# Spectra loads in the places of the copied products, tied to blocks, in the product stage of a two-layer MetaFormer kernel

## The chip, the cores and the metric

The kernel runs on one core of one Trainium2 chip. The metric is the device time in microseconds of one execution; the median of several is compared. The engines go by the profile's names: PE (TensorE matmuls), PEld (its weight loads), DVE (VectorE), ACT (ScalarE), POOL (GpSimd) and SP (SyncE, which here only issues DMAs).

## What is computed

The input is 16 images of 128 channels by 32 x 32, float32. Two layers follow each other, each a token mixer and a channel mixer with residual additions. Layer 0 is linear attention, then a spectral unit; layer 1 is a pair of 3 x 3 convolutions, then a routed feed-forward part with 64 experts. The stage that the change touches is the core of the spectral unit:

```python
Vf = jnp.fft.rfft(phi, n=n, axis=0)
Uf_p = jnp.fft.rfft(u, n=n, axis=1)
Uf_m = jnp.fft.rfft(u * sgn3, n=n, axis=1)
U_plus = jnp.fft.irfft(Vf[None, :, :, None] * Uf_p[:, :, None, :], n=n, axis=1)[:, :sl]
U_minus = jnp.fft.irfft(Vf[None, :, :, None] * Uf_m[:, :, None, :], n=n, axis=1)[:, :sl]
...
out = jnp.einsum('btkd,k,kde->bte', U_plus, s, Mpp)
out = out + jnp.einsum('btkd,k,kde->bte', U_minus, s, Mpm)
```

For every frequency the kernel forms one 128 x 128 complex matrix g, the sum over the filters of filter spectrum times mixing matrix, and multiplies the spectra of all 16 samples with it. That multiplication, frequency by frequency, is the product stage.

## The kernel before

Four stages follow each other: attention and forward transform of layer 0 (lines 220 to 773), the product stage (lines 776 to 896), the inverse transform with convolutions and routing of layer 1, and the expert part with the output. The forward transform leaves the spectra in a DRAM tensor `vd`; the product stage reads them from there and writes its results to the DRAM tensors `yd`, from which the next stage loads.

The product stage works in NCH = 16 chunks of frequencies, and each chunk c in NM = 4 blocks m. What a chunk needs:

- `xc`, the spectra of chunk c, in four loads of 256 KB, one for each four samples (`begin`, line 785; the DMA is line 793). Each has its own place, so the four loads of the next chunk can start as soon as POOL has read the four places.
- `v`, made from them by POOL: for each load two `tensor_tensor` (line 796) and one `tensor_scalar` (line 797) that stores a negated part. This document calls these three instructions "turns". There are two tiles `v`.
- `g`, the matrices of the chunk: `generate` (line 799) makes 16 matmuls on 4 PSUM banks, `collect` (line 810) copies the four banks to SBUF, by ACT (line 818) or DVE (line 816). A chunk needs eight generates. There are two tiles `g`.

A block (c, m) does in this order: two generates for chunk c + 1; the first collect; `combine` of the block before; the second collect; `multiply` (line 820), which writes one PSUM bank `py` with 32 matmuls from `v` and `g` of chunk c; ACT's copy of `py` to the SBUF tile `yt` (line 891). `combine` (line 855) is two DVE instructions (lines 858 and 859) that read `yt` and write sum and difference into `ys`. So the result of a block is combined within the block after it. When the fourth block of a chunk has been combined, `finish` (line 838) does four POOL instructions on `ys` (lines 843 to 846) and SP issues two stores of 512 KB to `yd` (line 850). In block (c, 0) finish of chunk c - 1 thus comes first on POOL, and then the turns for chunk c + 1.

The matmuls are float32; the profile counts two records for each `nc.tensor.matmul`, so a generate pair shows as 64 records and a multiply as 64.

PE, DVE, ACT and POOL run in the order of the program text: that is what `tc.manual_schedule(engines=PINNED)` does. SP is not among the pinned engines, and its order is the framework's: in the steady part the two stores of a chunk come first, then four loads that run one chunk ahead of the turns that POOL is doing, each load issued when POOL has finished with its place. `yt` has one place, the four `xc` have one each, and each of the five takes 2 KB per partition.

Of the kernel before, what the change touches and what calls it, by code (L numbers as in the profile page):

```python
# [8 lines left out]
F32 = mybir.dt.float32  # L9
AF = mybir.ActivationFunctionType  # L10
ALU = mybir.AluOpType
# [3 lines left out]
P = 128  # L15
B, C, H, W = 16, 128, 32, 32
# [15 lines left out]
NM = NQ // 2  # L32
NCH = 16
JL = 8
CW = 2 * 2 * NM * JL

BP = B // 4
# [3 lines left out]
RG = P // KR  # L41
# [4 lines left out]
PINNED = {  # L46
    mybir.EngineType.PE, mybir.EngineType.DVE, mybir.EngineType.Activation, mybir.EngineType.Pool,
}
# [21 lines left out]
def metaformer_kernel(ctx: ExitStack, tc: tile.TileContext, io: dict, out: bass.AP):  # L70
    nc = tc.nc
# [26 lines left out]
    for n, (g_, b_, m_, v_) in enumerate(((V_G1, V_B1, V_M1, V_V1), (V_G2, V_B2, V_M2, V_V2))):  # L98
# [15 lines left out]
                name=nc.get_next_instruction_name(), ins=[], outs=[], act_func_set_id=EXP_LN  # L114
# [61 lines left out]
    with ExitStack() as l0:  # L176
# [3 lines left out]
        vd = dram.tile([NCH, P, B, CW], F32, name="vd", tag="vd")  # L180
# [39 lines left out]
        with ExitStack() as a0:  # L220
# [537 lines left out]
            with tc.manual_schedule(engines=PINNED):  # L758
                for p in range(-reach, B):
                    next(preparing, None)  # L760
                    for name, d in period:
                        b = p + d
# [13 lines left out]
        with ExitStack() as g0:  # L776
            gpl = [g0.enter_context(tc.tile_pool(name="gpl0", bufs=1))]
            cpl = g0.enter_context(tc.tile_pool(name="cpl", bufs=2, reuse_waits="tile"))
            gpl.append(g0.enter_context(tc.tile_pool(name="gpl1", bufs=1, reuse_waits="tile")))
            xcl = g0.enter_context(tc.tile_pool(name="xcl", bufs=1, reuse_waits="tile"))  # L780
            psg = g0.enter_context(tc.tile_pool(name="psg", bufs=8, space=PSUM, reuse_waits="tile"))
            gs, vs = {}, {}
            NB = EPR // 4

            def begin(c):

                v = cpl.tile([P, 2 * NM * JL, 3, B], F32, name="v", tag="v")
                vs[c] = v
                vv = v.rearrange("p (x w) k b -> p x k b w", x=2)
                for i in range(B // BP):  # L790
                    bs = slice(i * BP, (i + 1) * BP)
                    xc = xcl.tile([P, BP, 2, 2, NM * JL], F32, name="xc", tag=f"xc{i}")
                    nc.sync.dma_start(xc.rearrange("p b x r w -> p b (x r w)"), vd[c, :, bs, :])
                    e, o = (xc[:, :, x].rearrange("p b r w -> p r b w") for x in range(2))
                    for x, op in enumerate((ALU.add, ALU.subtract)):
                        nc.gpsimd.tensor_tensor(vv[:, x, 1:, bs], e, o, op)  # L796
                    nc.gpsimd.tensor_scalar(v[:, :, 0, bs], v[:, :, 2, bs], -1.0, None, ALU.mult)  # L797

            def generate(c, q):

                pg = [psg.tile([P, 4, CW], F32, name="pg", tag="p") for r in range(RG)]
                for i in range(4):
                    for r in range(RG):
                        rs = slice(r * KR, (r + 1) * KR)
                        nc.tensor.matmul(  # L805
                            pg[r][:, i], mst[rs, 4 * q + i, :], ph[rs, c, :], start=True, stop=True,
                        )
                return pg

            def collect(c, q, pg):  # L810

                for r in range(RG):
                    dst = gs[c].rearrange("p w (g q i) -> p g q w i", g=RG, q=NB)[:, r, q]
                    src = pg[r].rearrange("p i w -> p w i")
                    if r % 2 and (r == 1 or q % 2 or c == 0):
                        nc.vector.tensor_copy(dst, src)  # L816
                    else:
                        nc.scalar.copy(dst, src)  # L818

            def multiply(c, m, x, py, fresh):  # L820

                g, v = gs[c], vs[c]
                for kl in range(JL // RG):
                    for ri in range(2):
                        for grp in range(RG):
                            jl = RG * kl + grp
                            rows = slice(grp * 2 * B, (grp + 1) * 2 * B)

                            nc.tensor.matmul(  # L829
                                py[rows, x, kl, :],  # L830
                                v[:, (x * NM + m) * JL + jl, 1 - ri : 3 - ri, :]
                                .rearrange("p k b -> p (k b)"),
                                g[:, ((x * 2 + ri) * NM + m) * JL + jl, :],
                                start=(grp not in fresh), stop=(ri == 1), skip_group_check=True,
                            )
                            fresh.add(grp)

            def finish(c, ys):

                eng = nc.gpsimd if c + 1 < NCH else nc.vector  # L840
                e = cpl.tile([P, JL // RG, 2, C], F32, name="ye", tag="ye", bufs=1)
                yv = ys[:, :, 0]
                eng.tensor_tensor(e, yv[:, :, :2], yv[:, :, 2:], ALU.add)  # L843
                eng.tensor_tensor(yv[:, :, 2:], yv[:, :, :2], yv[:, :, 2:], ALU.subtract)  # L844
                eng.tensor_tensor(yv[:, :, 0], e[:, :, 0], e[:, :, 1], ALU.add)
                eng.tensor_tensor(yv[:, :, 1], e[:, :, 0], e[:, :, 1], ALU.subtract)
                for kl in range(JL // RG):
                    last = c + 2 >= NCH
                    j0 = kl * RG + (c - NCH + 2 if last else c) * JL
                    nc.sync.dma_start(  # L850
                        yd[last][j0 : j0 + RG].rearrange("g r b x e -> (g r b) (x e)"),
                        ys[:, kl].rearrange("p x m e -> p (x m e)"),
                    )

            def combine(c, m, ys, t):

                a, b = t
                nc.vector.tensor_tensor(ys[:, :, 0, m], b, a, ALU.add)
                nc.vector.scalar_tensor_tensor(ys[:, :, 1, m], b, -1.0, a, ALU.mult, ALU.add)
                if m == NM - 1:  # L860
                    finish(c, ys)

            with tc.manual_schedule(engines=PINNED):
                begin(0)
                gs[0] = gpl[0].tile([P, CW, C], F32, name="g", tag="g")
                for q in range(NB):
                    collect(0, q, generate(0, q))
                waiting = None
                for c in range(NCH):
                    if c + 1 < NCH:  # L870
                        gs[c + 1] = gpl[(c + 1) % 2].tile([P, CW, C], F32, name="g", tag="g")

                    ys = cpl.tile([P, JL // RG, 2, NM, C], F32, name="ys", tag="ys")
                    for m in range(NM):
                        if c + 1 < NCH:
                            pg = [generate(c + 1, 2 * m + x) for x in range(2)]
                            collect(c + 1, 2 * m, pg[0])
                        if waiting:
                            combine(*waiting)
                        if c + 1 < NCH:  # L880
                            if m == 0:
                                begin(c + 1)
                            collect(c + 1, 2 * m + 1, pg[1])
                        py = psg.tile([P, 2, JL // RG, C], F32, name="py", tag="p")
                        fresh = set()
                        for x in range(2):
                            multiply(c, m, x, py, fresh)
                        if c + 1 < NCH or m == 0:
                            t = cpl.tile([P, 2, JL // RG, C], F32, name="yt", tag="yt", bufs=1)
                        if c + 1 < NCH:  # L890
                            nc.scalar.copy(t, py)
                            waiting = c, m, ys, (t[:, 0], t[:, 1])
                        else:
                            nc.scalar.copy(t[:, m % 2], py[:, 0])
                            waiting = c, m, ys, (t[:, m % 2], py[:, 1])
                combine(*waiting)


    gpool = ctx.enter_context(tc.tile_pool(name="gpool", bufs=1))
# [10 lines left out]
    with ExitStack() as c1:  # L910
# [562 lines left out]
        with tc.manual_schedule(engines=PINNED | {mybir.EngineType.SP}):  # L1473
# [4 lines left out]
            bs = w1[:, C, :].rearrange("(k r i) h -> r k i h", r=2, i=EG)  # L1478
# [137 lines left out]
        with tc.manual_schedule(engines=PINNED):  # L1616
            yt = first.tile([P, 2, N], F32, name="yt", tag="v")
            for pr in (0, 7, 1, 2, 3, 4, 5, 6):
# [8 lines left out]
                for j in range(2):  # L1627
                    b = 2 * pr + j
                    if j and pr % 2:
                        t = yt[:, pr // 2 % 2]  # L1630
# [160 lines left out]
```

## Time and profile before

| what | value |
| --- | --- |
| time, median of 3 executions | 1241.78 us (1241.42 to 1245.75) |
| time of the profiled execution | 1238.85 us |
| its span | 1237.1 us |
| granted TensorE clock, mean | 0.992 |
| line 829, multiply: first start to last start | 395.7 to 652.6 us |
| turns, first to last start | 386.9 to 645.0 us |
| copy of `py` to `yt` (line 891) | 0.586 us |
| combine (lines 858 and 859), median | 0.451 and 0.952 us |
| turns of one load: lines 796, 796, 797, median | 0.741, 0.741 and 0.851 us |
| finish (lines 843 to 846), median | 1.397, 1.268, 0.731 and 0.919 us |
| load of `xc`: KB, issue to landing | 256, 3.4 us (2.9 to 5.6) |
| store to `yd`: KB, issue to landing | 512, 3.6 us |

The span is the time from the first to the last recorded work of that one execution; the device time holds a little more around it. A median over instructions mixes those that run beside others and those that run alone: lines 858 and 859 take from 0.411 to 0.977 us. "Issue to landing" runs from SP's instruction to the last signal of the transfer.

### The profile page before, as it was taken

The numbers are of one execution on the slowest core, as the hardware profiler recorded it, in microseconds if no ns is written. First come the engines' busy times: TensorE is split into PE (matmuls) and PEld (weight loads), VectorE is DVE, ScalarE is ACT, GpSimd is POOL, SyncE is SP. The second block draws the span as 40 slices with busy tenths as digits, with TensorE's granted clock in tenths as the row PEclk, the third lists the DMA queues.
The fourth block names the chain that finished last, engine by engine and source line by source line (L and its number), as shares of the span: only waits on it lengthen the run. The fifth ranks groups of instructions, "written<-read, shape, count | busy, mean of one in ns | idle before, by whom it ended". The sixth has DMA issues, their size and how long they took to land.

```text
span 1237.1 us, 34361 instructions
## 1 busy us (share of the span) xinstructions
PE 1160.6 (94%) x14398; PEld 953.9 (77%) x14398; DVE 936.6 (76%) x1944; ACT 725.1 (59%) x1420; POOL 603.4 (49%) x800
## 2 busy tenths in 40 slices
PE   7889999999999999999997999999999999998996
PEld 6677777777767988988887888898888888885453
DVE  5888888888766777776674689898988989885235
ACT  4777787777655777777770445555555555544211
POOL 2435454655568788888793433343443333230003
PEclk9999999999999999999998999999999999999998
DMA  7005334353436344333348612223233321416899
GB/s 281 24 31 168 120 116 154 97 171 100 154 120 197 98 140 140 128 128 128 108 140 274 153 52 52 85 88 119 84 120 120 103 86 68 154 34 218 323 403 384
DMA packets 91243, 175.14 MB, mean 142 GB/s; under 512 B 5968, under 2 KB 42064, under 8 KB 90448
## 3 DMA queue, kind: packets, MB, share of 16 engines
q1 hardware_dynamic: 90448, 170.46, 41.2%
q0 software_dynamic: 640, 2.49, 0.6%
q8 instruction: 113, 1.85, 0.6%
q14 instruction: 42, 0.34, 0.1%
HBM read 110.28 MB, written 62.65 MB: 140 GB/s over the span
## 4 chain that ended last, share of the span: by engine, by line
PE 38%; DVE 22%; POOL 17%; issue 13%; ACT 5%; DMA 4%; SPq 0%; POOLq 0%; DVEq 0%; ACTq 0%
PE pcv L988 10%; POOL v L796 7%; PE big L638 6%; DVE bst L135 4%; POOL v L797 4%; PE big L171 3%; PE big L152 3%; PE big L570 3%; PE big L450 2%; PE big L533 2%; PE big L432 2%; PE py L829 2%; POOL ye L843 1%; DVE abss L1231 1%; POOL ys L844 1%
## 5 line engine op out<-in xcount | busy, mean ns | idle before, releaser
L988 PE MATMUL pcv<-v,cw 128*128 128x256 f32 x1152 | 258.2, 380 | 1.4 <-POOL v L1178 1.4
L988 PEld LDWEIGHTS pcv<-v,cw 128*128 128x128 f32 x1152 | 214.7, 190 | 34.5 <-issue 4.9
L818 ACT COPY g<-pg 128x512 f32<-128x512 f32 x316 | 161.1, 605 | 45.3 <-PE pg L805 44.6
L816 DVE COPY g<-pg 128x512 f32<-128x512 f32 x196 | 127.7, 682 | 72.0 <-PE pg L805 72.0
L805 PE MATMUL pg<-ph,mst 32*128 32x128 f32 x4096 | 143.0, 279 | 9.4 <-issue 7.9
L805 PEld LDWEIGHTS pg<-ph,mst 32*128 32x128 f32 x4096 | 127.9, 186 | 25.4 <-issue 16.3
L829 PE MATMUL py<-g,v 128*32 128x128 f32 x4096 | 124.8, 274 | 1.9 <-POOL v L797 1.7
L829 PEld LDWEIGHTS py<-g,v 128*32 128x32 f32 x4096 | 108.0, 110 | 9.9 <-POOL v L797 2.3
L144 ACT ACTIVATE tok<-tok,sts 128x128 f32<-128x128 f32 x256 | 101.9, 480 | 16.9 <-DVE sts L1065 13.6
L135 DVE BATCH_NORM_STATS2 bst<-big 128x6 f32<-128x256 f32 x256 | 91.2, 418 | 20.9 <-PE big L152 11.7
L796 POOL TENSOR_TENSOR v<-xc 128x256 f32<-128x256 f32 x128 | 99.0, 798 | 3.3 <-PE pg L805 2.3
L638 PE MATMUL big<-u,mu 128*128 128x128 f32 (+4 forms) x384 | 86.0, 380 | 0.0
L1178 POOL TENSOR_TENSOR v<-abss 128x256 f32<-128x256 f32 x64 | 49.1, 787 | 68.1 <-DVE abss L1174 56.7
L286 POOL TENSOR_TENSOR xf<-ab 128x256 f32<-128x256 f32 x34 | 24.8, 728 | 110.2 <-DVE ab L253 110.2
L1197 POOL TENSOR_TENSOR yo<-abss 128x256 f32<-128x256 f32 x32 | 23.5, 735 | 108.6 <-DVE abss L1193 108.6
L638 PEld LDWEIGHTS big<-u,mu 128*128 128x128 f32 x384 | 56.7, 191 | 18.0 <-issue 15.4
L570 PE MATMUL big<-wf,ub 128*128 128x256 f32 x256 | 62.0, 385 | 0.2
L144 ACT ACTIVATE tt<-tt,sts 128x128 f32<-128x128 f32 x128 | 51.1, 481 | 14.6 <-DVE sts L1065 14.6
L797 POOL TENSOR_SCALAR v<-v 128x256 f32<-128x256 f32 x64 | 55.6, 868 | 5.6
L475 POOL TENSOR_TENSOR ke<-ke,ks 128x1024 f32<-128x1024 f32 x16 | 30.6, 1914 | 55.1 <-DVE qs L483 43.4
L570 PEld LDWEIGHTS big<-wf,ub 128*128 128x128 f32 x256 | 46.2, 190 | 8.8 <-ACT xn L423 3.0
L144 ACT ACTIVATE ub<-ub,sts 128x128 f32<-128x128 f32 x128 | 50.8, 481 | 0.0
(256 smaller groups left out, 2478.9 us busy)
## 6 DMA issues: line engine op xcount, KB each, us to landing
we<-in_weight SPq DMA_DIRECT2D x32, 1024.0 KB, 9.3
xc<-vd SPq DMA_DIRECT2D x64, 256.0 KB, 3.4
yd<-ys SPq DMA_DIRECT2D x32, 512.0 KB, 3.6
vd<-xf SPq DMA_DIRECT2D x15, 1024.0 KB, 5.1
y<-yd SPq DMA_DIRECT2D x15, 896.0 KB, 6.3
x<-in_x SPq DMA_DIRECT2D x16, 512.0 KB, 5.3
mi<-in_M_phi SPq DMA_DIRECT2D x16, 512.0 KB, 4.7
xd<-x SPq DMA_DIRECT2D x16, 512.0 KB, 6.3
```

The lines of the kernel that those rows point to most:

```text
L135: nc.vector.bn_stats(bst[:, j : j + 2, :].rearrange("p j s -> p (j s)"), src[:, j : j + 2, :].rearrange("p j c -> p c j"),)
L144: nc.scalar.activation(dst[:, j, :], src[:, j, :], AF.Identity, bias=nm[:, j : j + 1], scale=r[:, j : j + 1],)
L570: nc.tensor.matmul(dst, self.ub[:, q, :], wf[:, q, :], start=True, stop=True)
L638: nc.tensor.matmul(self.pa[:, a:hi], mu[:, NF - 1 - si, tap, :], self.u[:, a - tap : hi - tap], start=(tap == 0), stop=(tap == KU - 1),)
L796: nc.gpsimd.tensor_tensor(vv[:, x, 1:, bs], e, o, op)
L797: nc.gpsimd.tensor_scalar(v[:, :, 0, bs], v[:, :, 2, bs], -1.0, None, ALU.mult)
L805: nc.tensor.matmul(pg[r][:, i], mst[rs, 4 * q + i, :], ph[rs, c, :], start=True, stop=True,)
L816: nc.vector.tensor_copy(dst, src)
L818: nc.scalar.copy(dst, src)
L829: nc.tensor.matmul(py[rows, x, kl, :], v[:, (x * NM + m) * JL + jl, 1 - ri : 3 - ri, :] .rearrange("p k b -> p (k b)"), g[:, ((x * 2 + ri) ...
L988: nc.tensor.matmul(pc[:, i], wt[:, dy, k, :], v[:, k, dy * WT : dy * WT + HT], start=(dy == 0), stop=(dy == 2),)
L1178: nc.gpsimd.tensor_tensor(v[:, k, WT : WT + HT], self.ab[:, 0], self.ab[:, 1], op)
```

## The change

Three things are altered, all in the product stage.

First, the places. The pool `xcl` of four places and the single place of `yt` are replaced by a pool `ring` of five places r0 to r4, which is as much memory. `yt` of block m takes place r0, r1, r2 or r3 by m. The four loads take r2, r3, r4 and r1. So three of the places are used in turn by a copied product and by a load: a load then waits until DVE has combined the product that was there, and a copy waits until POOL has read the load that was there.

Second, the order. SP joins the pinned engines, so that its DMAs are issued in the order of the text. `begin` is split into `fetch` (one load) and `turns` (the three POOL instructions for it). In block 0 of chunk c come loads 1 and 2 of chunk c + 1, then finish of chunk c - 1 with its stores, then turns 0, 1 and 2; in block 2 load 3 and turns 3; in block 3 load 0 of chunk c + 2.

Third, `finish` is called from the loop and no longer from `combine`.

```diff
-            xcl = g0.enter_context(tc.tile_pool(name="xcl", bufs=1, reuse_waits="tile"))
+            ring = g0.enter_context(tc.tile_pool(name="ring", bufs=1, reuse_waits="tile"))
...
-            def begin(c):
-
-                v = cpl.tile([P, 2 * NM * JL, 3, B], F32, name="v", tag="v")
-                vs[c] = v
+            xcs = {}
+
+            def fetch(c, i):
+
+                if c < NCH:
+                    xc = ring.tile([P, BP, 2, 2, NM * JL], F32, name="xc", tag=f"r{(2, 3, 4, 1)[i]}")
+                    bs = slice(i * BP, (i + 1) * BP)
+                    nc.sync.dma_start(xc.rearrange("p b x r w -> p b (x r w)"), vd[c, :, bs, :])
+                    xcs[c, i] = xc
+
+            def turns(c, i):
+
+                if c >= NCH:
+                    return
+                if i == 0:
+                    vs[c] = cpl.tile([P, 2 * NM * JL, 3, B], F32, name="v", tag="v")
+                v = vs[c]
                 vv = v.rearrange("p (x w) k b -> p x k b w", x=2)
-                for i in range(B // BP):
-                    bs = slice(i * BP, (i + 1) * BP)
-                    xc = xcl.tile([P, BP, 2, 2, NM * JL], F32, name="xc", tag=f"xc{i}")
-                    nc.sync.dma_start(xc.rearrange("p b x r w -> p b (x r w)"), vd[c, :, bs, :])
-                    e, o = (xc[:, :, x].rearrange("p b r w -> p r b w") for x in range(2))
-                    for x, op in enumerate((ALU.add, ALU.subtract)):
-                        nc.gpsimd.tensor_tensor(vv[:, x, 1:, bs], e, o, op)
-                    nc.gpsimd.tensor_scalar(v[:, :, 0, bs], v[:, :, 2, bs], -1.0, None, ALU.mult)
+                bs = slice(i * BP, (i + 1) * BP)
+                xc = xcs.pop((c, i))
+                e, o = (xc[:, :, x].rearrange("p b r w -> p r b w") for x in range(2))
+                for x, op in enumerate((ALU.add, ALU.subtract)):
+                    nc.gpsimd.tensor_tensor(vv[:, x, 1:, bs], e, o, op)
+                nc.gpsimd.tensor_scalar(v[:, :, 0, bs], v[:, :, 2, bs], -1.0, None, ALU.mult)
...
-                if m == NM - 1:
-                    finish(c, ys)
-
-            with tc.manual_schedule(engines=PINNED):
-                begin(0)
+
+            with tc.manual_schedule(engines=PINNED | {mybir.EngineType.SP}):
+                for i in range(B // BP):
+                    fetch(0, i)
+                for i in range(B // BP):
+                    turns(0, i)
+                fetch(1, 0)
...
                         if c + 1 < NCH:
-                            if m == 0:
-                                begin(c + 1)
                             collect(c + 1, 2 * m + 1, pg[1])
+                        if m == 0:
+                            fetch(c + 1, 1)
+                            fetch(c + 1, 2)
+                            if waiting:
+                                finish(*waiting[::2])
+                            for i in range(3):
+                                turns(c + 1, i)
+                        elif m == 2:
+                            fetch(c + 1, 3)
+                            turns(c + 1, 3)
+                        elif m == 3:
+                            fetch(c + 2, 0)
...
                         if c + 1 < NCH or m == 0:
-                            t = cpl.tile([P, 2, JL // RG, C], F32, name="yt", tag="yt", bufs=1)
+                            t = ring.tile([P, 2, JL // RG, C], F32, name="yt", tag=f"r{m}")
...
                 combine(*waiting)
+                finish(*waiting[::2])
```

## The prediction

> **What bounds the kernel now.** I read the page first, then the busy times of the product stage, then TensorE's waits and its timeline there, then the DMA view in narrow windows. The change lies between about 383 and 657 us. The steady part, from the second block of chunk 0 to the last block of chunk 14, reads:
>
> ```profile
> PE 1160.6 (94%) x14398; PEld 953.9 (77%) x14398; DVE 936.6 (76%) x1944; ACT 725.1 (59%) x1420; POOL 603.4 (49%) x800
> 401.01:643.03 242.02, 233.57 (x7428) 211.87 (x7425) 175.42 (x291) 181.69 (x349) 196.66 (x229) 1.00 0.39 125
> ```
>
> The second line is the stage: length, then busy PE, PEld, DVE, ACT, POOL, the clock and the DMA share. PE is busy 233.6 of 242.0 us at full clock, POOL only 196.7. What stops PE:
>
> ```profile
> PE pg L805 <- issue: 7.9, 13, 1.1
> PE py L829 <- POOL v L797: 1.7, 2, 1.2
> ```
> ```profile
> POOL ye L843 <- DVE ys L858: 38.1, 14, 6.1
> POOL v L796 <- DMA xc<-vd: 1.0, 1, 1.0
> ```
>
> (waiting line, releaser: us in total, times, longest.) PE hardly ever waits for `v`, and POOL waited for a load once. The largest stop is "issue", PE waiting for nothing the profile shows. The chain of waits runs along POOL here, but POOL itself waits 38.1 us for DVE, so that chain has slack. PE's timeline around one stop, chunk 8:
>
> ```profile
> 534.35 2.07 PE L805 MATMUL pg<-ph,mst 32*128 32x128 f32 x64
> 536.35 1.96 PE L829 MATMUL py<-g,v 128*32 128x128 f32 x64
> 538.23 0.82 PE L805 MATMUL pg<-ph,mst 32*128 32x128 f32 x17
> 540.02 1.62 PE L805 MATMUL pg<-ph,mst 32*128 32x128 f32 x47 [0.97 <-issue]
> ```
>
> An undisturbed block is 3.88 us (one generate pair, one multiply). Here PE stops after 17 of 64 matmuls. Reading the starts of all L829 groups so, 58 blocks take 242.0 us where 58 x 3.88 is 225.0: **17.0 us are lost**, and by block of a chunk: m=0 2.8, m=1 1.8, m=2 0.3, m=3 12.1 (0.32 to 1.49 in each of chunks 1 to 13, mean 0.92). So the loss sits in the block after SP's burst:
>
> ```profile
> 533.38 0.80 SPq L850 DMA_DIRECT2D yd<-ys  x2
> 534.95 7.80 SPq L793 DMA_DIRECT2D xc<-vd  x4
> ```
>
> and what rides on the same DMA engines is the instruction stream. Three DMA answers: the whole stage, 534.0 to 536.9, and 537.5 to 537.7:
>
> ```profile
> q8 instruction: 62, 1.02, 1.5%
> ```
> ```profile
> q1 hardware_dynamic: 274, 1.04, 94.6%
> ```
> ```profile
> q8 instruction: 1, 0.02, 29.1%
> ```
>
> 62 packets of 16 KB for 64 blocks: one per block. During the stores of `yd` the engines are full and no q8 packet moves; it comes at 537.6, 5.6 us after the one before (532.0, found the same way) instead of one block, 3.88. In nine disturbed chunks PE goes on 2.23 to 2.48 us after that packet's start, mean 2.35. This is an inference from timing; the profile names no releaser.
>
> **What the Trainium skill says.** "Runtime: NRT & Kernel Launch", section on instruction fetch mechanics: instructions come in 16 KiB blocks over a DMA queue which the sequencer drives itself, fetching the next while the current one executes, mostly hidden. The trace agrees on size and queue; hidden it is not here. "DMA: Bandwidth & Descriptors", section on queues, rings and completion order: each engine alternates between queues only after draining a whole packet. The trace agrees so far that q8 does not overtake: measured from the issue of `yd`, its packet starts after 3.41 to 4.87 us in chunks 1 to 13 (mean 4.06), while the two stores take about 3.5.
>
> **The change, part by part.** The compiled order of PE, DVE, ACT and POOL is the same before and after, instruction for instruction; PE's and DVE's waits differ at most in which DMA semaphore is named. Only SP's order, the places and the waits tied to them change. That finish stands ahead of the next turns in the source moves nothing: POOL ran it first already.
>
> *(1) The burst is broken up.* Before, SP issued two 512 KB stores and then four 256 KB loads for the chunk after next, the first 1.57 us behind the stores, just when PE crosses into a new instruction block (535.0 in chunk 8). After, per chunk: loads 1 and 2 in block 0, the stores after finish, load 3 in block 2, load 0 of the next in block 3. The fetch behind the stores then has no load in front of it. The stores stay, so I take the short delays of before, 3.4 to 3.8 us after the store issue, which went with losses of 0.32 to 0.78: 0.45 instead of 0.92. 13 x 0.47 = **6.1 us saved**. Bounds: 0 if the stores alone hold it, 12 if all goes.
>
> *(2) The loads' new places.* Each load waits for DVE's combine of its block. Combine ends 3.37 us after a block's start (L859 at 536.77 for 0.95, block at 534.35), so SP issues at 3.45; data flow from 1.0 to 2.6 us behind an issue, i.e. 0.55 to 2.15 into the next block, and PE asks there at about 0.6. That holds a fetch by up to 0.6 us, and an undisturbed fetch has 0.6 to spare (its packet 2.95 ahead of need, 2.35 needed): nothing for load 3 and load 0. Loads 1 and 2 come together at 2.7 and 3.0 of block 0 (POOL idle, combine shorter): up to 0.6 to 0.9 late, 0 to 0.3 lost, I take 0.1. Before, m=0 to 2 lost 4.9; after, 14 x 0.1 plus 0.5 of scatter is 1.9: **3.0 saved**. Bounds: 4.9 saved, or three losses of 0.5 a chunk, 16 lost.
>
> *(3) The new wait on load 3.* `v` of the next chunk is complete only after turns 3, which now follow a load of the same chunk. From the start of block 2: issue 3.45, landing 3.4 (page, median of xc) is 6.85; turns 3 take 2.67 (540.72 to 543.39) less 0.1 of queueing: 9.4. PE needs `v` at 2 x 3.88 + 2.0 = 9.76. Slack 0.36, and 0.45 more when block 3 stalls. POOL, now waiting about 0.4, has behind it only the next finish, whose input comes at 15.5 + 2.3; ends at 17.2: fine. Price 0 in the steady part. Nothing is queued on SP behind load 3 but load 0. Landings range from 2.9 to 5.6, the long ones behind the stores; at load 3 the stores are 4.4 us old and done.
>
> *(4) Four places for `yt`.* ACT's copy no longer needs the previous combine done, but the profile shows no such wait. It now waits for turns 0 and 1 in blocks 2 and 3: those end 2.5 and 5 us ahead. Nothing either way.
>
> *(5) The last chunk* has no generate, so its first multiply comes at 7.76, while `v` is ready at 9.4: 1.6 lost where before PE lost about 0.95 (start 644.9 to 645.87). **0.6 more.**
>
> Sum: -6.1 - 3.0 + 0.6 = -8.5, of which I take 8 as the scatter is not all mine to remove. The profiled execution took 1238.85 (span 1237.1), 2.9 below the median shown; 1230.9 against it is **1234** against 1241.78.
>
> **The rivals.** *A, the stores alone hold the fetch.* Then block 3 keeps its 0.92, and of (2) some 1.5 remain, less 0.6: -1, 1241. For it: the engines are full during the stores alone. Against: the delay splits into about 3.4 to 3.8 and 3.9 to 4.9, as if the first load were sometimes ahead. *B, load 3 is the new end (slower).* If it lands after 5.2 us, as loads do behind the stores, turns 3 end at 11.2 where PE can wait until 10.2: 1.0 a chunk, 15 us, less the 8: 1249. It decides from a landing of 4.2. Against: the DMA is idle then. *C, every fetch gap goes:* -17 + 0.6, 1225. *D, the tied loads meet the fetch in every chunk:* 1.5 + 0.45 instead of 1.17, 11 us: 1253. For it: one block of chunk 9 lost 0.96 with a single load beside the fetch.
>
> **How the numbers follow.** Forecast 0.48 (its own range 1229 to 1239), A 0.24, C 0.10, B 0.12, D 0.06. Within 0.5% means within 6.2 us, about what a measurement of this kernel can tell from no change. Of the forecast 0.35 lies below 1235.6; with C and 0.02 of A, faster is 0.47; same 0.13 + 0.22 = 0.35; slower B and D, 0.18. The range 1225 to 1245 leaves out B and D.
>
> **What would show it.** Right: 58 blocks in about 233 us, "issue" on L805 near 3, block 3 near 4.3 us, q8 3.4 to 3.8 us behind the stores. POOL waits on xc about 0.4 in every chunk (6 in total) and PE on `v` at most 1.5 us, in the last chunk. Wrong: PE waiting for POOL `v` in most chunks (B), block 3 still 0.9 over (A), new stops in blocks 0 to 2 (D).

## The result, and the profile after

| kernel | median of its runs | runs |
| --- | --- | --- |
| before | 1243.12 us (1237.74 to 1249.64) | 17 |
| after | 1237.53 us (1234.66 to 1241.47) | 17 |

The ratio is 0.9959, 95% interval 0.9942 to 0.9976: the change takes about 5 us off where 8 were forecast. That lies inside the 0.5% which the prediction counts as no change and to which it gave 0.35, against 0.47 for a larger gain. The profiled execution took 1234.8 us, with a span of 1233.0 us, which is 4.1 less than before. Read along the span, the 4.1 are made up so: the multiply of block (0, 1) starts 0.7 later (401.68 instead of 401.01), the 58 blocks of the steady part are 5.15 shorter, from there to SP's first load of the next stage's `y` it is 0.6 longer (22.43 instead of 21.85), and the rest differs by 0.2. So the gain lies in the stage that was changed. This is the steady part of the kernel after (length, busy PE, PEld, DVE, ACT and POOL, clock, DMA share, GB/s):

```profile
401.68:638.55 236.87, 233.34 (x7428) 212.02 (x7424) 174.27 (x291) 181.48 (x349) 197.78 (x229) 1.00 0.38 129
```

The waits of PE and of POOL from 395 to 652 us in the kernel after (us in total, times, longest):

```profile
PE pg L816 <- issue: 4.5, 12, 1.1
PE py L840 <- issue: 2.1, 1, 2.1
PE py L840 <- POOL v L808: 0.9, 1, 0.9
```
```profile
POOL ye L854 <- DVE ys L869: 19.9, 12, 1.9
POOL v L807 <- DMA xc<-vd: 10.7, 7, 4.3
```

Stops for "issue" on the generate line fell from 7.9 to 4.5. PE waits for `v` once only, in the last chunk. POOL now waits for loads: twice at the start of the stage, for 3.6 and 4.3 us, and five times for 0.54 to 0.59 us before turns 3, as the tie of load 3 makes it do. PE feels nothing of the five. But the stops have not only shrunk, they have moved. PE's timeline in chunk 8 of the kernel after:

```profile
529.61 2.07 PE L816 MATMUL pg<-ph,mst 32*128 32x128 f32 x64
531.61 1.95 PE L840 MATMUL py<-g,v 128*32 128x128 f32 x64
533.49 0.82 PE L816 MATMUL pg<-ph,mst 32*128 32x128 f32 x17
534.68 1.62 PE L816 MATMUL pg<-ph,mst 32*128 32x128 f32 x47 [0.37 <-issue]
536.22 1.95 PE L840 MATMUL py<-g,v 128*32 128x128 f32 x64
538.11 2.07 PE L816 MATMUL pg<-ph,mst 32*128 32x128 f32 x64
```

and SP's timeline of the same chunk:

```profile
528.36 0.80 SPq L792 DMA_DIRECT2D xc<-vd  x2
532.50 1.55 SPq L861 DMA_DIRECT2D yd<-ys  x2
537.25 7.73 SPq L792 DMA_DIRECT2D xc<-vd  x3
```

The generates at 529.61, 533.49 and 538.11 open blocks 1, 2 and 3. Here block 2 stops (the next multiply starts 4.61 after the one before instead of 3.88), two blocks behind loads 1 and 2, and block 3, the one that had the stop before, runs through. Counted as the prediction counted it, from the starts of the multiply groups and as time over 3.88 us:

| lost in the steady part, us | m=0 | m=1 | m=2 | m=3 | all |
| --- | --- | --- | --- | --- | --- |
| before | 2.8 | 1.8 | 0.3 | 12.1 | 17.0 |
| after | 0.5 | 0.9 | 3.1 | 7.4 | 11.8 |

### The profile page after: what moved, and what is told of

Same layout as the page of the kernel before. It is cut to its first block, busy times and chain, and to the rows that moved or that the text cites. A ratio compares the mean times of both kernels' runs of the same rounds, so it can differ in the third digit from the quotient of the medians.

```text
span 1233.0 us, 34413 instructions
## 1 busy us (share of the span) xinstructions
PE 1160.1 (94%) x14398; PEld 953.7 (77%) x14398; DVE 935.7 (76%) x1944; ACT 724.8 (59%) x1420; POOL 604.0 (49%) x800
## 4 chain that ended last, share of the span: by engine, by line
PE 57%; DVE 22%; issue 11%; ACT 5%; DMA 4%; POOL 1%; SPq 0%; POOLq 0%; ACTq 0%; DVEq 0%
PE pg L816 10%; PE py L840 10%; PE pcv L1012 10%; PE big L638 7%; DVE bst L135 4%; PE big L171 3%; PE big L152 3%; PE big L570 3%; PE big L450 2%; PE big L533 2%; PE big L432 2%; DVE abss L1255 1%; DVE xp L1277 1%; DVE xp L1139 1%; ACT tt L144 1%
## 5 line engine op out<-in xcount | busy, mean ns | idle before, releaser
L840 PE MATMUL py<-g,v 128*32 128x128 f32 x4096 | 126.7, 276 | 3.6 <-issue 2.1
L840 PEld LDWEIGHTS py<-g,v 128*32 128x32 f32 x4096 | 109.8, 111 | 11.7 <-issue 2.4
L144 ACT ACTIVATE tok<-tok,sts 128x128 f32<-128x128 f32 x256 | 101.9, 480 | 16.9 <-DVE sts L1089 13.6
L135 DVE BATCH_NORM_STATS2 bst<-big 128x6 f32<-128x256 f32 x256 | 91.0, 416 | 20.8 <-PE big L152 11.7
L914 ACT COPY yt<-py 128x512 f32<-128x512 f32 x60 | 35.1, 585 | 27.9 <-ACT g L829 17.2
```

The costliest lines, as they stand in the source:

```text
L135: nc.vector.bn_stats(bst[:, j : j + 2, :].rearrange("p j s -> p (j s)"), src[:, j : j + 2, :].rearrange("p j c -> p c j"),)
L144: nc.scalar.activation(dst[:, j, :], src[:, j, :], AF.Identity, bias=nm[:, j : j + 1], scale=r[:, j : j + 1],)
L840: nc.tensor.matmul(py[rows, x, kl, :], v[:, (x * NM + m) * JL + jl, 1 - ri : 3 - ri, :] .rearrange("p k b -> p (k b)"), g[:, ((x * 2 + ri) ...
```

## The experiments

All experiments change the product stage alone, save the fifth and the seventh. Ratios are to the kernel before, run beside them on the same chip. The losses are those of the profiled execution.

| label | ratio and 95% interval | steady part, us | lost in m=0 | m=1 | m=2 | m=3 |
| --- | --- | --- | --- | --- | --- | --- |
| e2_order_own_places | 1.0000 (0.9972 to 1.0027) | 237.8 | 2.0 | 0.1 | 0.2 | 10.5 |
| e2t_tied_own_places | 0.9968 (0.9951 to 0.9985) | 238.3 | 0.4 | 0.0 | 0.2 | 12.7 |
| e3_stores_later | 0.9911 (0.9881 to 0.9942) | 231.9 | 3.1 | 0.0 | 2.6 | 1.2 |
| e4_stores_behind_load3 | 1.0060 (1.0038 to 1.0083) | 249.1 | 19.1 | 0.5 | 4.3 | 0.1 |
| e5_wi_behind_y | 0.9965 (0.9948 to 0.9981) | 237.1 | 0.3 | 0.8 | 3.7 | 7.3 |
| e6_all_tied | 0.9871 (0.9842 to 0.9901) | 228.5 | 1.4 | 0.2 | 1.5 | 0.3 |
| e7_all_tied_wi | 0.9881 (0.9846 to 0.9917) | 228.4 | 0.7 | 0.3 | 2.3 | 0.0 |
| e9_load3_block1 | 0.9963 (0.9942 to 0.9983) | 238.9 | 0.3 | 0.1 | 0.9 | 12.5 |
| e10_stores_alone | 0.9935 (0.9906 to 0.9964) | 238.6 | 0.1 | 1.3 | 0.5 | 11.7 |

**The order without the shared places.** The loads and `yt` get places of their own, the order of the text stays:

```diff
-                    xc = ring.tile([P, BP, 2, 2, NM * JL], F32, name="xc", tag=f"r{(2, 3, 4, 1)[i]}")
+                    xc = ring.tile([P, BP, 2, 2, NM * JL], F32, name="xc", tag=f"xc{i}")
...
-                            t = ring.tile([P, 2, JL // RG, C], F32, name="yt", tag=f"r{m}")
+                            t = ring.tile([P, 2, JL // RG, C], F32, name="yt", tag="yt")
```

> The changed kernel's order of DMAs, but the four loads keep places of their own and yt keeps its single one, so a load waits only until POOL has read its place. Fetch theory (PE stops because the fetch of its next instruction block is held up behind SP's transfers): load 3 now follows the two stores at once and the others follow as POOL frees them, so the burst is back; block 3 again loses 0.9 us or more a chunk, 12 us or more in all, and the time is that of the kernel before, 1240 to 1248, ratio 0.998 to 1.005. Order theory (the text order alone, with finish and stores ahead, brings the gain): ratio stays at 0.996.

The time is that of the kernel before. Without the shared places nothing holds a load back but POOL's reading of its place. In chunk 8 the stores go out at 533.52 and data flow from 534.34 to 542.65 without a gap, stores and loads in one burst as before. Its profile doesn't fit its time well: the steady part is 4.2 us shorter than before, and the part behind the stage, from the end of the last multiply to the end of the span, 5.2 longer. That part takes 580.3 to 589.5 us in the profiles of kernels that leave it unchanged, so one profile decides nothing there. Block 3 loses 0.81 a chunk in chunks 1 to 13, where 0.9 or more was expected. What this run shows is that the order of the text alone brings no gain in time that could be measured.

**The tie without the shared places.** To the last kernel a 4-byte DMA on SP is added ahead of the loads, which waits for ACT's first copy of `g` in that block:

```diff
+            def tie(c, m):
+
+                if c + 1 < NCH:
+                    nc.sync.dma_start(mark[c : c + 1, m : m + 1], gs[c + 1][0:1, 0, 8 * m : 8 * m + 1])
...
                         if m == 0:
+                            tie(c, m)
                             fetch(c + 1, 1)
                             fetch(c + 1, 2)
...
                         elif m == 2:
+                            tie(c, m)
                             fetch(c + 1, 3)
...
                         elif m == 3:
+                            tie(c, m)
                             fetch(c + 2, 0)
```

> As the run with own places and the order of the text, but three times a chunk (blocks 0, 2 and 3) SP first issues a DMA of 4 bytes that waits for ACT's first copy of g in that block, about 1.9 us into it; loads 1 and 2, load 3 and load 0 of the next chunk come behind it. yt has one place. Fetch theory: the loads flow from 2.9 to 4.5 us of a block, behind the block's own fetch and ahead of the next, so they hold up nothing; block 2 loses 0 where the changed kernel lost 3.1 in all, block 3 still loses about 0.5 a chunk behind the stores, and the ratio is 0.994 to 0.997. Places theory (four places for yt, and PSUM freed sooner, bring the gain): with one place it is gone, 0.999 to 1.001.

In time the gain is back, at 0.9968 with one place for `yt`: the median is 1237.17 us, and 1241.68 in the kernel just above, run beside it. So the ties bring a gain of this size without the shared places. It is not a wide margin, as the two intervals against the kernel before overlap, and the profiles don't show where the gain lies: the steady parts are 238.3 here and 237.8 there. Loads 1 and 2, now issued earlier in block 0, no longer stop block 2 (0.2 instead of 3.1). The expectation for block 3 was missed, with 0.88 a chunk in chunks 1 to 13 where 0.5 was expected. Load 3, issued at 535.30 in chunk 8 and so 2 us earlier than in the kernel after, was suspected and is tried apart next.

**The stores alone.** Two kernels take the loads away from the stores, one after the other. In the first, load 3 moves to block 1, ahead of the stores, which become a function of their own, `store`:

```diff
+                        elif m == 1:
+                            tie(c, m)
+                            fetch(c + 1, 3)
+                            if 0 < c < NCH - 1:
+                                store(*held)
                         elif m == 2:
-                            tie(c, m)
-                            fetch(c + 1, 3)
                             turns(c + 1, 3)
```

> This is e2t_tied_own_places (own places for the loads, one yt, tied loads 1 and 2 in block 0) with only load 3 moved: it is tied in block 1 instead of block 2, so that the stores of block 1 have no load behind them. The stores themselves stay where they were (issued when POOL's finish is done, about 2.9 us into block 1). Theory 'a load issued soon behind the stores adds to the hold-up': block 3 falls from 12.7 us (0.9 a chunk) to 6 to 7 (0.4 to 0.5), the steady part is 231.5 to 234. Rival 'the stores alone hold the fetch': block 3 stays at 11 to 13 us, the steady part at 237 to 239.

Block 3 stays at 12.5. But in chunk 8 the load goes out at 534.47 and the stores at 535.25, so a load is still beside them, ahead instead of behind. The second moves it to block 3, a chunk earlier:

```diff
                         elif m == 1:
-                            tie(c, m)
-                            fetch(c + 1, 3)
                             if 0 < c < NCH - 1:
                                 store(*held)
...
                             fetch(c + 2, 0)
+                            fetch(c + 2, 3)
```

> As e9_load3_block1 (own places for the loads, one yt, stores issued by SP when POOL's finish is done), but load 3 runs with load 0 in block 3, tied to ACT's first copy of g there, so that no load is issued within 2.5 us before or after the stores. Theory 'the loads near the stores, ahead of them or behind them, make half of the hold-up': block 3 falls to 6 to 8 us (0.4 to 0.6 a chunk), the steady part is 231.5 to 234.5 and the time about 1233. Rival 'the stores alone hold the fetch': block 3 stays at 11 to 13 us, the steady part at 237 to 239, and then the 0.57 a chunk of the changed kernel comes from something else than the loads' distance.

The rival holds: 11.7 in block 3, with nothing beside the stores. SP's timeline of e10_stores_alone around chunk 8:

```profile
528.31 0.79 SPq L798 DMA_DIRECT2D xc<-vd  x2
533.01 0.80 SPq L870 DMA_DIRECT2D yd<-ys  x2
540.62 0.24 SPq L791 DMA_DIRECT2D mark<-g  x1
```

PE's timeline there:

```profile
533.97 2.07 PE L822 MATMUL pg<-ph,mst 32*128 32x128 f32 x64
535.97 1.95 PE L846 MATMUL py<-g,v 128*32 128x128 f32 x64
537.86 0.82 PE L822 MATMUL pg<-ph,mst 32*128 32x128 f32 x17
539.38 1.62 PE L822 MATMUL pg<-ph,mst 32*128 32x128 f32 x47 [0.70 <-issue]
```

The generates open blocks 2 and 3; block 3 stops. The DMA view of the same kernel, first from 533.9 to 537.0, then from 537.0 to 537.3:

```profile
q1 hardware_dynamic: 277, 1.01, 82.0%
```
```profile
q8 instruction: 1, 0.02, 19.4%
```

Each line is a queue with packets, MB and its share of the engines' time. The stores take 82% of the engines' time and no instruction packet moves; it comes at 537.09, within 0.01 us of their last packet and 5.38 after the one before (531.71). That one came 1.6 us into its block, as undisturbed ones do; here this would be 535.6. So the packet is 1.5 late, and block 3 loses 1.07 of that, which the timeline shows in part as the stop of 0.70.

The time from such a packet to PE's going on is the same in all kernels. In the steady parts of the nine kernels in which PE stops for "issue" for more than 0.3 us, it does so 73 times and goes on 2.17 to 2.88 us after the start of a q8 packet, 2.34 in the mean and in 70 cases below 2.6. The profile still names no releaser, so the link is a reading of times, but one that holds wherever the stop is moved.

In the kernel before, e2_order_own_places, e2t_tied_own_places, e9_load3_block1 and e10_stores_alone the stores go out about 2.9 us into block 1, and block 3 loses 10.5 to 12.7 us, whatever loads lie near. In single chunks a load close behind may add to it: from the issue of the stores to the packet it is at most 4.11 us in e10_stores_alone, and up to 5.43 in e2_order_own_places, where the first load follows within 0.9 us.

This fits the 7.4 in the kernel after, too. There, loads 1 and 2 hold the fetch before it to 532.48, PE stops in block 2, and what PE asks for next it asks for that much later, while the stores, which follow POOL, stay where they are. In chunk 8 after, block 2 loses 0.74 and block 3 nothing; in chunk 13, block 2 loses nothing and block 3 1.13. Over chunks 1 to 13 the correlation of block 3's loss with that of blocks 1 and 2 is -0.91 (-0.90 in e5_wi_behind_y below, which has the same product stage). Per chunk, blocks 2 and 3 together lose 0.94 before, 0.78 after, 0.84 in e10_stores_alone and 0.90 in e2t_tied_own_places. So the stop seems to be paid once, early or late. This is argued from the traces: no run moves loads 1 and 2 and nothing else.

**The stores moved.** Two kernels move the stores against PE's blocks; all else stays as in the kernel after. In the first they come in block 2 ahead of load 3, behind a 4-byte DMA that waits for the copy of block 1; in the second they follow load 3 and wait for nothing else:

```diff
                         elif m == 2:
+                            if 0 < c < NCH - 1:
+                                nc.sync.dma_start(mark[c : c + 1, :], waiting[3][0][0:1, 0, 0:1])
+                                store(*held)
                             fetch(c + 1, 3)
                             turns(c + 1, 3)
```
```diff
                         elif m == 2:
                             fetch(c + 1, 3)
+                            if 0 < c < NCH - 1:
+                                store(*held)
                             turns(c + 1, 3)
```

> The changed kernel with the stores to yd of chunks 0 to 13 put behind a DMA of 4 bytes that waits for ACT's copy of yt of block 1: SP issues them about 0.85 us into block 2, 1.8 us later than now, same bytes. Load 3 follows them. Fetch theory: their data flow from 1.7 to 4.4 us of block 2, behind that block's fetch and ahead of the next one; block 3 loses 0 to 0.1 a chunk instead of 0.57, so 58 blocks take 229 to 232 us instead of 236.9 and the time is 5 to 7 us below the changed kernel's: ratio 0.990 to 0.992. Rival (PE stops for banks that DVE and ACT free late, or for anything but transfers): PE, ACT, DVE and POOL do the same, 236 to 238 us, ratio 0.995 to 0.997.

> The changed kernel with the stores of chunks 0 to 13 issued right behind load 3, about 3.8 us into block 2, 4.8 us later than now, same bytes. Fetch theory: load and stores lie together in front of the fetch that PE asks for 0.6 us into block 3 and needs 0.6 us into the next block 0; it starts at about 3.5 us of block 3 instead of 1.5, so block 0 loses 1.0 to 1.3 a chunk (14 to 18 us in all), while block 3 loses nothing: 58 blocks take 241 to 246 us, ratio 1.000 to 1.006. Rival (transfers do not stop PE): 236 to 238 us, ratio 0.995 to 0.997.

Both came out as expected but for the size of the second's loss, 19.1 in block 0 and 249.1 us where at most 18 and 246 were expected. The steady parts, e3_stores_later first, then e4_stores_behind_load3:

```profile
403.32:635.24 231.92, 230.92 (x7428) 210.66 (x7424) 168.28 (x291) 181.50 (x349) 194.49 (x229) 1.00 0.40 132
```
```profile
404.40:653.49 249.09, 234.19 (x7428) 212.54 (x7425) 168.31 (x291) 181.50 (x349) 194.66 (x229) 1.00 0.36 120
```

Same work and, but for 4 bytes a chunk, same bytes, 17.2 us apart by the moment of two stores. In e3_stores_later the stores of chunk 8 go out 1.9 us later than in the kernel after:

```profile
534.15 0.24 SPq L912 DMA_DIRECT2D mark<-yt  x1
534.44 0.79 SPq L865 DMA_DIRECT2D yd<-ys  x2
```

Their data start at 535.26, and the instruction packet of that block came at 534.93, just ahead; the next, at 538.96, was again in time, 1.65 into its block. In e4_stores_behind_load3 the stores meet the fetch of the following block. SP, then PE:

```profile
478.10 0.32 SPq L792 DMA_DIRECT2D xc<-vd  x1
478.47 0.90 SPq L864 DMA_DIRECT2D yd<-ys  x2
```
```profile
478.86 2.07 PE L816 MATMUL pg<-ph,mst 32*128 32x128 f32 x64
480.86 1.95 PE L840 MATMUL py<-g,v 128*32 128x128 f32 x64
482.74 0.93 PE L816 MATMUL pg<-ph,mst 32*128 32x128 f32 x19
484.79 1.61 PE L816 MATMUL pg<-ph,mst 32*128 32x128 f32 x45 [1.12 <-issue]
```

The packet due at about 480.5 came at 482.41, and PE stops in the next block, block 0 of the following chunk. So where the stores fall in PE's blocks sets most of the loss. A load can hold a packet as well: in six chunks of e3_stores_later it comes 2.4 to 2.6 us into block 3, in the middle of load 3's data, and the next block 0 loses 0.24 to 0.72, together 2.9 of the 3.1 us in the table.

**Everything tied.** The kernel with own places and ties, with the stores tied as well, to ACT's first copy of `g` in block 2, and load 3 tied in block 1. Against e9_load3_block1 only the stores differ:

```diff
                         elif m == 1:
                             tie(c, m)
                             fetch(c + 1, 3)
+                        elif m == 2:
+                            tie(c, m)
                             if 0 < c < NCH - 1:
                                 store(*held)
-                        elif m == 2:
                             turns(c + 1, 3)
```

> Own places for the loads and one for yt, and every transfer tied to ACT's first copy of g, about 1.9 us into a block: loads 1 and 2 in block 0, load 3 in block 1, the two stores in block 2, load 0 of the next chunk in block 3. Fetch theory: no transfer lies in front of a fetch, 58 blocks take 226 to 229 us (225.0 undisturbed), PE's issue stops in the steady part are under 1 us in all, and the ratio is 0.985 to 0.990, below that of the run with the later stores. Rival (something besides transfers costs the last 5 to 7 us): 231 to 233 us, 0.990 to 0.993.

The steady part of e6_all_tied, PE's wait for "issue", and SP around one pair of stores:

```profile
403.39:631.85 228.46, 228.19 (x7428) 209.17 (x7424) 170.94 (x291) 181.51 (x349) 195.66 (x229) 1.00 0.41 134
```
```profile
PE pg L822 <- issue: 0.2, 1, 0.2
```
```profile
544.95 0.32 SPq L798 DMA_DIRECT2D xc<-vd  x1
548.50 0.24 SPq L791 DMA_DIRECT2D mark<-g  x1
548.84 0.96 SPq L870 DMA_DIRECT2D yd<-ys  x2
```

PE is busy 228.2 of 228.5 us: the stage runs at PE's own pace. It is 3.4 us above 58 x 3.88; what makes these up is not shown. The instruction packets come at 548.48, before the stores' data (549.66 to 552.49), and at 552.76, right behind them and in time. By its ratio this is the best kernel of the study, 0.9871 (0.9842 to 0.9901); the interval overlaps that of e3_stores_later, and the steady part is 3.5 us shorter. From e9_load3_block1 to it the steady part falls by 10.4 us, by the stores' place alone.

**The handoff to the next stage.** In the kernel after, PE stops for 2.1 us in the last chunk (the wait on L840 above), at the time of the 1 MB load of `wi`, which SP issues at 641.01. The instruction packet comes at 645.02, 7.29 after the one before, and PE goes on 2.28 later. The load of `wi` is moved to POOL's queue, behind the first load of `y` there:

```diff
-        nc.sync.dma_start(wi, wid)
...
+                if b == 0:
+                    nc.gpsimd.dma_start(wi, wid)
```

> The changed kernel with the 1 MB load of wi for the next stage taken off SP, where it is issued during the last chunk, and put on POOL's queue behind the first loads of that stage. Theory that the last chunk's stops are again the instruction fetch behind a transfer: PE's stop of 2.1 us in the last chunk and the 3.4 us at half clock that follow it go. Two readings of what that is worth. If PE sets the end of the stage: 3 to 4 us less than the changed kernel, ratio 0.992 to 0.993. If the transfers still to be drained there (stores of the last two chunks, first loads, wi) set it: 0 to 1 us less, ratio 0.995 to 0.997.

> The run with every transfer tied, and the load of wi moved as in the run of that alone. Expected 0 to 4 us below the run with every transfer tied, by the same two readings: 3 to 4 if PE sets the end of the stage, 0 to 1 if the drain does.

The last chunk's multiplies in the kernel after, then in e5_wi_behind_y:

```profile
641.05 4.15 PE L840 MATMUL py<-g,v 128*32 128x128 f32 x141 [0.54 <-DVE pooled L927]
647.30 5.13 PE L840 MATMUL py<-g,v 128*32 128x128 f32 x115 [2.10 <-issue]
```
```profile
640.69 7.40 PE L840 MATMUL py<-g,v 128*32 128x128 f32 x256 [0.34 <-DVE pooled L927]
```

The stop is gone and the last pair of stores goes out from 651.48 instead of 655.82, yet SP's first load of `y` starts at 662.1 instead of 661.0, and the time is the same (0.9965 against 0.9959). What SP waits for there, between 630 and 672 us, in e5_wi_behind_y and then in e6_all_tied:

```profile
SPq L1034 <- DMA yd<-ys: 9.3, 2, 5.0
```
```profile
SPq L1055 <- DMA yd<-ys: 7.7, 2, 6.6
```

In the kernel after it is 2.7 us, once. So this load waits for the stores to `yd` and not for PE. In e5_wi_behind_y the moved `wi`, issued at 647.48 and landed at 660.71, lies beside these stores, so this run alone doesn't tell what an earlier PE is worth. But e6_all_tied leaves `wi` on SP and shows the same: its last multiply ends 10.6 us before that of the kernel after, its load of `y` starts only 7.0 earlier, and 6.7 of that is the earlier end of the steady part. PE has no stop for "issue" in the last chunk of e6_all_tied, so e7_all_tied_wi had none to remove there, and it brings nothing (0.9881 against 0.9871). That the transfers still under way hold the stores was not tried apart. The steady part of e5_wi_behind_y, in which nothing was changed, repeats that of the kernel after to within 0.6 us in each of the four blocks.

## Why the prediction was right in direction and off in size

- **What bounds the stage: right.** Late instruction packets were most of the loss. With the transfers out of their way (e6_all_tied) "issue" falls to 0.2 us, and the steady part is 13.6 us shorter than before, where 17.0 were lost.
- **(1) The burst broken up: this step failed.** It said that "the fetch behind the stores then has no load in front of it" and priced block 3 at 0.45 instead of 0.92, 6.1 us saved. With no load near the stores block 3 still loses 0.81 a chunk (e10_stores_alone, chunks 1 to 13). What the step named as its proof did appear, block 3 at 0.57 and the packet 3.65 to 4.08 us behind the stores, but, by the account above, in good part because PE had stopped in block 2 already. Blocks 2 and 3 together went from 12.3 to 10.5: 1.8 saved, not 6.1. The step read the short delays of before, 3.4 to 3.8 us with small losses, as those without a load in front. In e10_stores_alone, with no load near, the delays of chunks 1 to 13 run from 3.71 to 4.11 and the losses from 0.24 to 1.13, so the spread doesn't show that; what makes it stays open.
- **(2) The loads' new places: right for two blocks.** Blocks 0 and 1 lost 4.6 before and 1.3 after, 3.3 saved against 3.0 for blocks 0 to 2. The price of loads 1 and 2, issued together, was 0.1 a chunk (bound 0.3) and measured 0.22, in block 2; as it spared block 3 about as much, it cost little in the end.
- **(3) The wait on load 3: right.** PE never waits for `v` in the steady part. POOL waits 0.54 to 0.59 us before turns 3 in five chunks, not 0.4 in each.
- **(4) The places for `yt`: right in price.** ACT does wait for POOL there (7.4 us in 14 waits), which the step had excluded; PE shows no wait for it.
- **(5) The last chunk: the right sum, by luck.** 0.6 was forecast for a wait on `v` and 0.6 measured, made up of a smaller wait on `v`, a stop of 2.1, and an earlier handoff.

The steps gave -8.5; the profile shows 1.8 + 3.3 saved, 0.6 lost at the end and 0.7 at the start, which no step had priced. The largest term came to less than a third of its size, and the direction is owed to step (2) more than to it. Rival A, "the stores alone hold the fetch", had the mechanism of block 3; its time was too high as it gave blocks 0 to 2 a gain of 1.5 only. Rival D's stops exist, in block 2, at 0.22 a chunk where D had 1.5 a chunk over three blocks. B and C did not happen.

## What to carry to other kernels

Where "issue" stops recur in a long unrolled loop, look up when the instruction packet is due and which large transfer lies there, and move that transfer by a fraction of a block; its moment can matter more than its size or its order. When a stop shrinks, add up the neighbouring blocks before calling it a gain: here 4.7 us less in block 3 came with 2.8 more in block 2. A marker that a forecast names should be one which the rival doesn't produce too.

## What had not been expected of the hardware

- Two stores of 512 KB keep the instruction packet back until they are through, though the profile counts them as 277 packets for 1.01 MB: it starts at 537.09, the stores' last packet at 537.08, in e10_stores_alone. The Trainium skill, "Runtime: NRT & Kernel Launch", section on instruction fetch mechanics, calls the cost of crossing a 16 KiB block mostly hidden; in this stage it is hidden in part (17.0 of 242.0 us lost before), almost wholly (3.4 of 228.5 in e6_all_tied), or costs 1.4 us a chunk in one block alone (19.1 us in 14 chunks of e4_stores_behind_load3), by when the stores go out.
- After the 2.1 us stop in the last chunk of the kernel after, the granted clock fell. The stretch from 645 to 660 us:

```profile
645.00:660.00 15.00, 12.90 (x156) 11.62 (x150) 4.31 (x10) 0.98 (x3) 2.74 (x5) 0.89 0.72 244
```

The clock is at 0.50 from 648.4 to 651.8 and at 1.00 on both sides, which makes the mean of 0.89. The Trainium skill, "TensorE: Matmul & The Clock Gate", part on the HAM clock gate, states a half rate after at least one idle window of about 3.4 us; here the fall followed a shorter stop. In e2t_tied_own_places and e10_stores_alone a stop of 2.0 us at the same place went with the same mean of 0.89. But a stop of 2.07 us in e2_order_own_places, which ended at 523.29, and one of 2.24 us in e4_stores_behind_load3, at 662.78, left the clock at 1.00. So the length of the stop alone doesn't decide; what does stays open.
